# A graph kernel's matrix passes: which operand is TensorE's weights, and how the matrix lies in DRAM

## Chip, core and metric

The kernel runs on one core of a Trainium2 chip. The metric is the time on the device in microseconds (us) of one execution; the median over several executions is given. Profiles are of one execution each.

## The reference

Four graph layers run one after the other on 6250 nodes of 64 features, over 206,250 edges sorted by destination (each node has also a self loop). All of them apply the same adjacency between nodes; only the third also uses data of the edges:

```python
h = relu(layernorm(x)); x = x + sgconv(relu(sgconv(h, W3, b3)), W4, b4)   # two applications of the adjacency
h = relu(layernorm(x)); x = x + D^-1/2 A D^-1/2 h                         # one
h = relu(layernorm(x)); x = x + edge_layer(h, edge_attr, src, dst)        # gather, gate, square, sum, root
h = relu(layernorm(x)); x = x + (h + P h + P P h + P P P h) / 4           # three (P = D^-1/2 A D^-1/2)
```

sgconv sums norm[src] * norm[dst] * x[src] into dst and multiplies by W. edge_layer turns each edge's 64 attributes by two small layers into a scale and a shift, applies them to a projected row Vp[src], and takes for each node the root of the mean of squares.

## The kernel before, in words

The kernel builds the matrix A of edge counts (6272 x 6272 bf16, nodes padded to NB = 49 blocks of 128) once, writes it to DRAM, and then applies it by TensorE. There are CS = 14 strips of CW = 448 destination columns, or NC = 7 chunks of W = 896 columns (CB = 7 blocks). A is symmetric, which the kernel checks during the edge stage. Features are split into three bf16 terms, U3 (or V3) of [128, 49, 3, 64], so that sums keep float32 precision.

The stages are these.

1. The beginning reads the edges, finds where each column begins, and builds the strips: one-hot comparisons on DVE (L935), counts by TensorE (L944), evictions to bf16 by ACT (L948), one DMA a strip (`A<-strip`, L956). The first application of A, `convolve`, runs on each strip while it is in SBUF.
2. Pass 1 and pass 2, both by `gather`, read the matrix back.
3. The edge stage takes 202 groups of 1024 edges. POOL issues eight indirect reads of `v` for each (L1238); PE, ACT and DVE compute the edge layers. In the gaps it compares blocks of A with their transposes (`piece` L1133, `crossed` L1137: PE transposes at L1150, DVE comparisons at L1156 against the tile `there`) and sums the first of the last three applications as far as node rows are done (`partial`, L1162, into Y).
4. The end finishes that first application with the last seventh of each strip (loop at L1412), and then calls `gather` twice (passes 3 and 4), the last of which writes the output.

`gather` (L972) works by strip: seven pieces of seven blocks are read by SP's queue (L980), and for each block `spread` (L736) multiplies three times: the weights are U3[:, b, k, :] (128 x 64), and A's block row (128 x 448) streams through. The three products alternate between the two halves of the PSUM partitions, so p_sum holds two partial sums of the transposed result, features by nodes. ACT evicts it to y (L983); `to_nodes` (L729) multiplies by `twice`, two identities above each other, which adds the halves and turns the chunk back to nodes by features (L733, in float32). p_sum has two buffers. Then a function for each pass goes on with the chunk: `convolved` (L995), `turned` (L1017, with PE work at L725, L1027, L1032), `propagated` (L1388). `split` (L705 to L709) makes the next U3.

The tile framework's scheduler sets the order on every engine, and tracks which buffer waits for which reader; only in the edge stage is the order on PE, ACT and DVE written out by hand (`slot`). [...] The pools for the pieces have 16 buffers of 784 KB in passes 1 and 2 and 12 in the end; a pass's pool is closed before the next one is opened.

Of the kernel before, what the change touches and what calls it, by code (L numbers as in the profile page):

```python
# [8 lines left out]
F32 = mybir.dt.float32  # L9
BF16 = mybir.dt.bfloat16  # L10
# [6 lines left out]
P = 128  # L17
# [598 lines left out]
def fast(ctx, tc, bad, x, src, dst, edge_attr, W3, b3, W4, b4, w1, b1, w2, b2, Bw, Bb, Cw, Cb,  # L616
# [7 lines left out]

    A = [dram.tile([P, NB, CW], BF16, name=f"A{c}") for c in range(CS)]
    pairs = dram.tile([EP + 512, 2], F32, name="pairs")
# [26 lines left out]
    def diagonal(m, name):  # L653
# [4 lines left out]
        return t  # L658

    node = ctx.enter_context(tc.tile_pool(name="node", bufs=1))  # L660
    stat = ctx.enter_context(tc.tile_pool(name="stat", bufs=2))
# [87 lines left out]
    with ExitStack() as ph:  # L749
# [70 lines left out]
        with ExitStack() as ps:  # L820
# [107 lines left out]
            for s in range(CS):  # L928
# [24 lines left out]
                for steps in beside:  # L953
                    for _ in steps:
                        pass
                nc.sync.dma_start(A[s], strip)  # L956
                beside = [convolve(s, strip)]
# [11 lines left out]

    PB = 7  # L970

    def gather(apool, wpool, psum, U3, then):  # L972

        for s in range(CS):
            if s % 2 == 0:
                y = wpool.tile([P, W], F32, name="y")
            p = psum.tile([P, 512], F32, name="p_sum", bufs=2)
            for k in range(NB // PB):
                t = apool.tile([P, PB, CW], BF16, name="piece")
                nc.sync.dma_start(t, A[s][:, k * PB:(k + 1) * PB, :])  # L980
                for b in range(PB):
                    spread(p, U3, k * PB + b, t[:, b, :], CW)
            nc.scalar.activation(y[:, s % 2 * CW:(s % 2 + 1) * CW], p[:, :CW], AF.Copy)  # L983
            if s % 2:
                then(s // 2, to_nodes(psum, y, CB))

    with ExitStack() as ph:
        wpool = ph.enter_context(tc.tile_pool(name="wpool", bufs=2))  # L990
        U3 = of_nodes(node)
        with tc.tile_pool(name="apool", bufs=16) as apool, \
                tc.tile_pool(name="ps1", bufs=1, space=PSUM) as psum:

            def convolved(c, y):  # L995
                z = wpool.tile([P, CB, D], F32, name="z")
                nc.scalar.activation(z, y, AF.Copy)
                add_whole(z, V3, c)
                nc.vector.tensor_mul(z, z, over_features(norm0[:, blocks(c)]))
                nc.vector.tensor_add(z, z, over_blocks(b4_r, CB))  # L1000
                nc.vector.tensor_add(X[:, blocks(c), :], X[:, blocks(c), :], z)
                h = wpool.tile([P, CB, D], F32, name="h")
                normed_and_split(h, U3, c, norm3)

            gather(apool, wpool, psum, V3, convolved)

# [6 lines left out]

        with tc.tile_pool(name="apool", bufs=16) as apool, \
                tc.tile_pool(name="ps2", bufs=1, space=PSUM) as psum:

            def turned(c, y):  # L1017
                z = wpool.tile([P, CB, D], F32, name="z")
                nc.vector.tensor_mul(z, y, over_features(norm3[:, blocks(c)]))
                nc.vector.tensor_add(X[:, blocks(c), :], X[:, blocks(c), :], z)  # L1020
# [8 lines left out]
                nc.vector.scalar_tensor_tensor(aT, aT, 0.2, aT, op0=OP.mult, op1=OP.max)  # L1029
                p_v = psum.tile([P, CB, D], F32, name="p_v", bufs=2)  # L1030
                for k in range(CB):
# [6 lines left out]

            gather(apool, wpool, psum, U3, turned)

# [8 lines left out]
    with ExitStack() as ph:  # L1049
# [83 lines left out]
        def piece(i, s):  # L1133
            held[s % 2] = piece_pool.tile([P, CB, CW], BF16, name="piece")
            nc.sync.dma_start(held[s % 2], A[s][:, blocks(i), :])

        def crossed(n, i, k, b):  # L1137
            if b % ROWS == 0:
                held["there"] = mpool.tile([P, ROWS, 2, CW], BF16, name="there", bufs=2)
                m = min(ROWS, CB - b)  # L1140
                for h in range(2):
                    nc.sync.dma_start(held["there"][:, :m, h, :],
                                      A[2 * i + h][:, k * CB + b:k * CB + b + m, :])

            p = ps_a.tile([P, 512], F32, name="p_sum", bufs=2).bitcast(BF16).rearrange(
                "p (a q) -> p a q", q=P)[:, :CB, :]
            for q in (slice(0, P),) if b != CB // 2 else (slice(0, D), slice(D, P)):
                half, lo = divmod(b * P + q.start, CW)
                for a in range(CB):
                    nc.tensor.transpose(p[q, a, :], held[half][:, a, lo:lo + q.stop - q.start],  # L1150
                                        ident_b)
            there = held["there"][:, b % ROWS].rearrange("p h w -> p (h w)")

# [225 lines left out]
    with ExitStack() as ph:  # L1379
        apool = ph.enter_context(tc.tile_pool(name="apool", bufs=12))  # L1380
        wpool = ph.enter_context(tc.tile_pool(name="wpool", bufs=2))
# [3 lines left out]
        for layer in range(3):  # L1385
# [23 lines left out]
            if layer:  # L1409
                gather(apool, wpool, psum, U3, propagated)  # L1410
            else:
                for s in range(CS):  # L1412
                    t = piece_pool.tile([P, CB, CW], BF16, name="piece")
                    nc.sync.dma_start(t, A[s][:, blocks(NC - 1), :])
                    p = psum.tile([P, 512], F32, name="p_sum", bufs=2)
                    for b in range(CB):
                        spread(p, U3, NB - CB + b, t[:, b, :], CW, NB - CB, CB)
                    nc.vector.tensor_add(Y[:, s, :], Y[:, s, :], p[:, :CW])
                    if s % 2:
                        propagated(s // 2, to_nodes(  # L1420
                            psum, Y[:, s - 1:s + 1, :].rearrange("p s w -> p (s w)"), CB))
# [42 lines left out]
```

## Time and profile before

| | us |
|---|---|
| timed, median of 3 | 4243.05 (4241.24 to 4245.13) |
| the profiled execution | 3727.58 |
| its span | 3725.9 |
| pass 1 (614.14 to 832.44) | 218.30 |
| pass 2 (835.05 to 1082.46) | 247.41 |
| edge stage (1124 to 3226) | 2102.00 |
| first layer of the end | 47.53 |
| passes 3 and 4 | 420.64 |

The profiled execution is 515 us shorter than the timed ones. Its page gives for the whole span PE 3092.7 us busy (83%), DVE 1890.3 (51%), POOL 1666.7 (45%), ACT 1282.9 (34%), and a mean granted TensorE clock of 0.905. Matmul spans overlap in the pipeline: a group's busy time is the time that at least one of them was under way, and its mean is that of one, with its way through the array. DMAs moved 650.35 MB in 278,027 packets; those of the matrix's pieces (`piece<-A`, 498 of 784 KB) took a median of 8.7 us from issue to landing, those of the strips (`A<-strip`, 14 of 5488 KB) 16.5 us.

### The profile page before, as it was taken

What the parts mean: (1) busy time and instruction counts of PE and PEld (TensorE: products, weight loads), DVE (VectorE), ACT (ScalarE), POOL (GpSimd) and SP (SyncE); (2) the same over time, 40 slices, a digit from 0 to 9 for tenths busy, and PEclk for the clock granted to TensorE, in tenths of its full rate; (3) what the DMA queues carried; (4) which work ended last, traced back from release to release, by engine and by line L of the source; (5) the groups of instructions that cost most, each with busy time, mean ns of one, the idle gap of its engine ahead of it and who ended that gap; (6) DMA issues with size and microseconds to landing.
All of it is one profiled execution on the core that took longest, in us unless ns stands there. A gap on an engine that the chain in (4) does not pass through costs nothing.

```text
span 3725.9 us, 57673 instructions
## 1 busy us (share of the span) xinstructions
PE 3092.7 (83%) x23299; PEld 1853.5 (50%) x23299; DVE 1890.3 (51%) x3525; ACT 1282.9 (34%) x2108; POOL 1666.7 (45%) x1870
## 2 busy tenths in 40 slices
PE   0499998999967777888878788787888887799999
PEld 0366665555544444444444444454444444466665
DVE  5999992221214555555655655555555565530100
ACT  0477772001103334433433443443443443210000
POOL 4100000000006777777777777777777777400000
PEclk9999998999987887888888888888888888899999
DMA  3244445968894333344344334334333433499997
GB/s 108 82 183 183 182 184 245 421 270 334 332 188 142 87 88 83 104 110 129 87 119 121 103 104 119 105 102 119 103 108 107 129 104 99 147 350 376 355 357 310
DMA packets 278027, 650.35 MB, mean 175 GB/s; under 512 B 106506, under 2 KB 158788, under 8 KB 275700
## 3 DMA queue, kind: packets, MB, share of 16 engines
q1 hardware_dynamic: 220036, 584.91, 43.4%
q0 software_dynamic: 54112, 58.92, 8.1%
q8 instruction: 185, 3.03, 0.3%
q10 hardware_dynamic: 3600, 2.73, 0.3%
q14 instruction: 94, 0.76, 0.1%
HBM read 562.82 MB, written 83.58 MB: 173 GB/s over the span
## 4 chain that ended last, share of the span: by engine, by line
PE 35%; POOL 32%; issue 14%; DMA 9%; DVE 8%; ACT 2%; POOLq 0%; DVEq 0%; ACTq 0%; SPq 0%
POOL v L1238 32%; PE p_sum L742 26%; DMA v<-Vp_dram,src_g 6%; PE p_a L944 3%; PE p_node L733 2%; DVE hd L935 1%; DVE lo L935 1%; PE p_bc L1264 1%; DMA dst_g<-in_dst 1%; DMA piece<-A 1%; DVE m L1273 0%; DVE m L1274 0%; PE p_node L915 0%; DVE junk L849 0%; PE p_node L725 0%
## 5 line engine op out<-in xcount | busy, mean ns | idle before, releaser
L1238 POOL DMA_INDIRECT v<-Vp_dram,src_g x1616 | 1606.2, 994 | 529.1 <-issue 460.8
L742 PE MATMUL p_sum<-piece,U 128*64 128x448 bf16 x10290 | 1051.7, 360 | 20.0 <-issue 9.9
L742 PEld LDWEIGHTS <-U 128*64 128x64 bf16 x12348 | 694.9, 111 | 527.5 <-issue 95.5
L1264 PE MATMUL p_bc<-BC,h 128*128 128x256 f32 x1616 | 603.6, 509 | 0.0
L1273 DVE TENSOR_TENSOR m<-gate,v 128x512 f32<-128x512 f32 x202 | 140.0, 693 | 798.1 <-DMA v<-Vp_dram,src_g 567.5
L1260 PE MATMUL p_bc<-BC_b,ones 3*128 3x512 bf16 x404 | 182.0, 450 | 359.4 <-DVE m L1274 358.8
L1280 ACT ACTIVATE m<-m 128x512 bf16<-128x512 f32 x202 | 127.3, 630 | 990.7 <-DVE m L1275 990.7
L1090 POOL MEMSET origin<- 128x1 f32 (+1 forms) x194 | 6.5, 96 | 970.8 <-PE p_sum L742 970.8
L1264 PEld LDWEIGHTS p_bc<-BC,h 128*128 128x128 f32 x1616 | 349.7, 240 | 157.6 <-issue 117.1
L1260 PEld LDWEIGHTS <-ones 3*128 3x128 bf16 x404 | 37.5, 93 | 613.6 <-DVE m L1274 486.2
L948 ACT ACTIVATE strip<-p_a 128x784 bf16<-128x784 f32 x392 | 301.7, 820 | 90.0 <-PE p_a L944 88.6
L1250 PE MATMUL p<-h,w_d 128*128 128x512 f32 x404 | 222.6, 633 | 50.7 <-ACT h L1254 50.7
L983 ACT ACTIVATE y<-p_sum 128x448 f32<-128x448 f32 x56 | 30.4, 543 | 678.1 <-PE p_sum L742 678.1
L1254 ACT ACTIVATE h<-p,b_c 128x512 f32<-128x512 f32 x404 | 255.0, 684 | 3.5 <-PE p L1250 3.4
L935 DVE TENSOR_TENSOR lo<-count,key 128x2048 bf16<-128x2048 bf16 x196 | 239.7, 1223 | 0.0
L742 PE MATMUL p_sum<-strip,U 128*64 128x448 bf16 x2058 | 236.2, 358 | 0.4 <-ACT strip L948 0.4
L1156 DVE SCALAR_TENSOR_TENSOR junk<-p_sum,there 128x896 bf16<-128x896 bf16 x196 | 212.3, 1083 | 12.1 <-PE p_e L1246 9.9
L944 PE MATMUL p_a<-hd,lo 128*128 128x98 bf16 x3136 | 189.5, 214 | 33.3 <-DVE lo L935 31.9
L1250 PE MATMUL p<-eT,w_d 128*128 128x512 f32 x404 | 212.3, 608 | 0.0
L944 PEld LDWEIGHTS <-lo 128*128 128x128 bf16 x3136 | 160.0, 101 | 103.4 <-DVE lo L935 81.5
L1391 DVE TENSOR_TENSOR z<-p_node,norm 128x448 f32<-128x448 f32 x21 | 13.1, 625 | 390.3 <-PE p_node L733 390.3
L1292 PE MATMUL p_s<-m,to 128*128 128x192 bf16 x1616 | 202.7, 278 | 1.1 <-DVE r_s L1300 0.4
(177 smaller groups left out, 3191.8 us busy)
## 6 DMA issues: line engine op xcount, KB each, us to landing
piece<-A SPq DMA_DIRECT2D x498, 784.0 KB, 8.7
A<-strip SPq DMA_DIRECT2D x14, 5488.0 KB, 16.5
e<-in_edge_attr SPq DMA_DIRECT2D x202, 256.0 KB, 2.8
v<-Vp_dram,src_g POOLq DMA_INDIRECT x1616
there<-A SPq DMA_DIRECT2D x56, 448.0 KB, 3.9
there<-A SPq DMA_DIRECT2D x56, 336.0 KB, 5.2
pairs<-pair SPq DMA_DIRECT2D x1, 1616.0 KB
Vp_dram<-v SPq DMA_DIRECT2D x7, 224.0 KB, 2.3
```

Of the source, the lines that this page charges most:

```text
L742: nc.tensor.matmul(p[half * D:(half + 1) * D, :w], U3[:, b, k, :], at_block, start=(i < 2), stop=(i >= 3 * n - 2))
L935: nc.vector.tensor_tensor(t, of.unsqueeze(1).to_broadcast(t.shape), key[:, k, at:at + GB].rearrange("p (h j) -> p h j", j=GQ) .unsqueeze(2 ...
L944: nc.tensor.matmul(p[:, j, :2 * NB], lo[:, g // GQ, :, g % GQ], hd[:, g // GQ, :, g % GQ], start=True, stop=True)
L948: nc.scalar.activation(strip[:, :, col:col + 2 * SG].rearrange("p b (j l) -> p b j l", l=2), p[:, :, :2 * NB].rearrange("p j (b l) -> p b ...
L1156: nc.vector.scalar_tensor_tensor(junk, p.rearrange("p a q -> p (a q)"), 0.0, there, op0=OP.add, op1=OP.not_equal, accum_out=unlike[:, n:n ...
L1238: nc.gpsimd.indirect_dma_start(out=v[:, j, :], out_offset=None, in_=Vp_dram[:, :], in_offset=bass.IndirectOffsetOnAxis(ap=src_g[:, g, j:j ...
L1250: nc.tensor.matmul(of[g][p], w, of[g].pop(x), start=True, stop=True)
L1254: nc.scalar.activation(of[g][t], of[g].pop(p), **how)
L1260: nc.tensor.matmul(p_bc[:, 4 * b:4 * b + 4].rearrange("p j o f -> p (j o f)"), ones, BC_b, start=True, stop=False)
L1264: nc.tensor.matmul(p_bc[:, 2 * q:2 * q + 2].rearrange("p j o f -> p (j o f)"), h2[:, q * P:(q + 1) * P], BC, start=False, stop=(k == 1))
L1273: nc.vector.tensor_mul(m, of[g].pop("gate"), of[g].pop("v"))
L1292: nc.tensor.matmul(p, to[:, :, j], m3[:, j].rearrange("p t f -> p (t f)"), start=(j == 0), stop=(j == J - 1))
```

## The change

The matrix lies in DRAM by chunks of 896 columns, not by strips of 448; a strip is written into half of a chunk's rows, and the edge stage's readers take it from there. `gather` works by chunk, with the roles of the operands exchanged: a block of A (128 x 128) is TensorE's weights, and the three terms of a block of U3, side by side (128 x 192), stream through. Since A is symmetric, the product is that of the chunk's own nodes, nodes by features, with the three terms in three columns of 64. Seven destination blocks accumulate in four PSUM banks, two to a bank (the last bank has one), over all 49 source blocks. Each bank is opened by a matmul of zeros that sets both halves, and all products then add to it. Four reduces on DVE add the three terms into z. p_acc has one buffer (the pool's default)[...]; p_v goes from two buffers to one. The eviction y and `to_nodes` leave `gather`, but stay in the loop of the first layer of the end, which now reads whole chunks from the deeper pool. Pieces are twice as large and half as many are held.

```diff
-    A = [dram.tile([P, NB, CW], BF16, name=f"A{c}") for c in range(CS)]
+    A = [dram.tile([P, NB, W], BF16, name=f"A{c}") for c in range(NC)]
+
+    def strip_of(s, bs):
+
+        return A[s // 2][:, bs, s % 2 * CW:(s % 2 + 1) * CW]
...
+    zeros = const.tile([P, 6 * D], BF16, name="zeros")
+    nc.vector.memset(zeros, 0.0)
...
-                nc.sync.dma_start(A[s], strip)
+                nc.sync.dma_start(strip_of(s, slice(0, NB)), strip)
...
-    def gather(apool, wpool, psum, U3, then):
-
-        for s in range(CS):
-            if s % 2 == 0:
-                y = wpool.tile([P, W], F32, name="y")
-            p = psum.tile([P, 512], F32, name="p_sum", bufs=2)
-            for k in range(NB // PB):
-                t = apool.tile([P, PB, CW], BF16, name="piece")
-                nc.sync.dma_start(t, A[s][:, k * PB:(k + 1) * PB, :])
-                for b in range(PB):
-                    spread(p, U3, k * PB + b, t[:, b, :], CW)
-            nc.scalar.activation(y[:, s % 2 * CW:(s % 2 + 1) * CW], p[:, :CW], AF.Copy)
-            if s % 2:
-                then(s // 2, to_nodes(psum, y, CB))
+    def gather(apool, psum, U3, then):
+
+
+        for c in range(NC):
+            p = psum.tile([P, 4, 512], F32, name="p_acc")
+            for k in range(NC):
+                t = apool.tile([P, CB, W], BF16, name="piece")
+                nc.sync.dma_start(t, A[c][:, blocks(k), :])
+                for d in range(CB):
+                    if k == 0 and d % 2 == 0:
+                        nc.tensor.matmul(p[:, d // 2, :6 * D], ident_b, zeros,
+                                         start=True, stop=False)
+                    for b in range(CB):
+                        nc.tensor.matmul(
+                            p[:, d // 2, d % 2 * 3 * D:(d % 2 + 1) * 3 * D],
+                            t[:, b, d * P:(d + 1) * P],
+                            U3[:, k * CB + b, :, :].rearrange("p t f -> p (t f)"),
+                            start=False, stop=(k == NC - 1 and b == CB - 1 and d in (1, 3, 5, 6)))
+            z = stat.tile([P, CB, D], F32, name="z")
+            for q in range(4):
+                n = min(2, CB - 2 * q)
+                nc.vector.tensor_reduce(
+                    z[:, 2 * q:2 * q + n, :],
+                    p[:, q, :n * 3 * D].rearrange("p (d t f) -> p d f t", t=3, f=D),
+                    axis=AX.X, op=OP.add)
+            then(c, z)
...
-        with tc.tile_pool(name="apool", bufs=16) as apool, \
+        with tc.tile_pool(name="apool", bufs=8) as apool, \
...
-                p_v = psum.tile([P, CB, D], F32, name="p_v", bufs=2)
+                p_v = psum.tile([P, CB, D], F32, name="p_v")
...
-            nc.sync.dma_start(held[s % 2], A[s][:, blocks(i), :])
+            nc.sync.dma_start(held[s % 2], strip_of(s, blocks(i)))
...
-                held["there"] = mpool.tile([P, ROWS, 2, CW], BF16, name="there", bufs=2)
+                held["there"] = mpool.tile([P, ROWS, W], BF16, name="there", bufs=2)
                 m = min(ROWS, CB - b)
-                for h in range(2):
-                    nc.sync.dma_start(held["there"][:, :m, h, :],
-                                      A[2 * i + h][:, k * CB + b:k * CB + b + m, :])
+                nc.sync.dma_start(held["there"][:, :m, :],
+                                  A[i][:, k * CB + b:k * CB + b + m, :])
...
-        apool = ph.enter_context(tc.tile_pool(name="apool", bufs=12))
+        apool = ph.enter_context(tc.tile_pool(name="apool", bufs=6))
...
                 for s in range(CS):
-                    t = piece_pool.tile([P, CB, CW], BF16, name="piece")
-                    nc.sync.dma_start(t, A[s][:, blocks(NC - 1), :])
+                    if s % 2 == 0:
+                        whole = apool.tile([P, CB, W], BF16, name="piece")
+                        nc.sync.dma_start(whole, A[s // 2][:, blocks(NC - 1), :])
+                    t = whole[:, :, s % 2 * CW:(s % 2 + 1) * CW]
```

## The prediction

> **What bounds the kernel now.** I read the page's slices first, for the stages, then the stretches of each stage, then the timeline of one chunk in the last passes, since a stage is decided by its own last wait.
>
> ```profile
> PE   0499998999967777888878788787888887799999
> PEclk9999998999987887888888888888888888899999
> DMA  3244445968894333344344334334333433499997
> GB/s 108 82 183 183 182 184 245 421 270 334 332 188 142 87 88 83 104 110 129 87 119 121 103 104 119 105 102 119 103 108 107 129 104 99 147 350 376 355 357 310
> ```
>
> One slice is 93 us. The four passes over the matrix are the slices with both PE and DMA near full: two near 614 to 1082 us, two at the end. The stretches say it exactly (length, then busy time of PE, PEld, DVE, ACT, POOL, clock, DMA share, GB/s):
>
> ```profile
> 614.14:832.44 218.30, 217.31 (x2156) 131.54 (x2156) 53.62 (x96) 19.58 (x38) 0.00 (x0) 0.99 0.87 357
> 835.05:1082.46 247.41, 242.14 (x2293) 142.93 (x2293) 44.65 (x77) 23.83 (x46) 0.00 (x0) 0.99 0.80 320
> 1124.00:3226.00 2102.00, 1681.14 (x8476) 977.49 (x8476) 1175.12 (x2312) 848.33 (x1447) 1605.83 (x1616) 0.85 0.39 107
> 3249.88:3297.41 47.53, 46.61 (x397) 30.02 (x397) 26.34 (x44) 6.92 (x12) 0.00 (x0) 0.95 0.91 330
> 3297.41:3718.05 420.64, 420.60 (x4309) 256.21 (x4308) 35.54 (x58) 24.43 (x44) 0.00 (x0) 1.00 0.92 357
> ```
>
> The last two passes have PE busy 420.60 of 420.64 us at full clock: **PE bounds them**, not the matrix reads, which were seen at 421 GB/s (slice 7) and run at 357 here. The timeline gives the period of a chunk (two strips), from 3297.41 to 3327.49 = 30.08 us:
>
> ```profile
> 3297.41 27.80 PE L742 MATMUL p_sum<-piece,U 128*64 128x448 bf16 x290
> 3325.14 0.88 PE L733 MATMUL p_node<-twice,y 128*128 128x64 f32 x6
> 3325.96 0.57 PE L742 MATMUL p_sum<-piece,U 128*64 128x448 bf16 x3
> 3326.45 1.11 PE L733 MATMUL p_node<-twice,y 128*128 128x64 f32 x8
> 3327.49 27.81 PE L742 MATMUL p_sum<-piece,U 128*64 128x448 bf16 x291
> ```
>
> So 294 matmuls of 448 columns take about 28.0 us, 95.3 ns each, and turning the chunk back to nodes (L733) about 2.0 us, with no idle: p_sum has two buffers, so the eviction (y, 0.54 us on ACT) runs under the next strip. The edge stage (2102 us) is paced by POOL: 1616 indirect reads of 994 ns and about 0.30 us of issue between them are 2091 us. It holds no gather.
>
> **The skill.** The Trainium skill, TensorE: Matmul & The Clock Gate, "Back-to-back issue gap", prices an isolated warm matmul at N/2.4 + 2.5 ns, but a stream of weight loads and matmuls at 81 ns for N=128 and 131 ns for N=512. This trace sides with the first: two 448-column matmuls on the two column halves take 190.6 ns, formula 189.2, and the weight-load streams below run at 56 ns for 128 columns. The same page, Part 1, says that the clock halves after about a 3.4 us window of idleness; here an idle PE of 2.25 to 2.75 us ahead of L1260 was followed by a slow matmul in 2 of 23 cases. PSUM — Partial Sum Buffer, "The four PSUM rules", says that a start flag clears the written-bits of the whole bank: two open groups can't each use one. That is why zeros open each bank; nothing in this trace shows it.
>
> **The change, part by part.**
>
> *Matmuls.* A chunk gets 7 pieces x 7 destination blocks x 7 source blocks = 343 matmuls of 192 columns, each with its own 128x128 weight load, for 294 of 448. The trace has this very shape at L1292, and 128-column ones at L1150:
>
> ```profile
> 3010.05 0.83 PE L1292 MATMUL p_s<-m,to 128*128 128x192 bf16 x8
> 3010.72 0.60 PE L1246 MATMUL p_e<-ident,e 128*128 128x128 f32 x4
> 3012.01 0.56 PE L1150 MATMUL p_sum<-ident_b,piece 128*128 128x128 bf16 x7
> 3012.40 1.08 PE L1250 MATMUL p<-h,w_d 128*128 128x512 f32 x2
> ```
>
> Eight of 192 take 0.67 us from start to start of the next group, 84 ns each with the change of group; seven of 128 take 0.39, 56 ns. The load is hidden. I take 82.5 ns (192/2.4 + 2.5): 343 x 0.0825 = 28.3 us. Bounds: 80 ns from below (the columns alone at the page's 2.4 GHz, 27.4 us); 89 ns from above (the page's stream prices interpolated, 30.5 us).
>
> *Zeros.* Four matmuls of 384 columns a chunk at 162 ns by the same formula: +0.65 us. Bounds 0.6 and 0.8.
>
> *Removed.* Both evictions of y and the 7 L733 products: −2.0 us of PE a chunk in all four passes (L733 stays in the first layer of the end).
>
> *The new wait.* p_acc fills four PSUM banks and has one buffer. In the changed program the first of the four reduces waits for the chunk's last matmul, and the next chunk's first zero load waits for the last reduce. So PE stands still meanwhile. The nearest row:
>
> ```profile
> L1300 DVE TENSOR_REDUCE r_s<-p_s 128x64 f32<-128x192 f32 x202 | 70.8, 351 | 0.2 <-PE p_s L1292 0.2
> ```
>
> 192 elements take 351 ns; the step from there to 448 in 617 ns (L694) is 1.04 ns an element, so 384 take about 550. Three of 550, one of 351, 0.04 us between: 2.13 us. The last matmul's drain (0.24 us from its start at L1292), 0.04 to DVE and 0.13 back to PE give 2.5 us less one slot: **2.48 us of idle PE a chunk**. Bounds: 2.2 (if the two-block reduce costs no second startup) and 3.2. Behind the wait on PE's queue stand the next chunk's 347 matmuls, in pass 2 also the transposes L725 and what follows; on SP's queue the next reads, which wait for PE to free pieces. Six or eight buffers of 4.0 us hold those: a piece of 1568 KB needs 3.8 us at 420 GB/s and its 49 matmuls 4.04, so DMA hides, as now. If the reads fell below 357 GB/s, they would pace it instead.
>
> A chunk then takes 28.3 + 0.65 + 2.48 = **31.43 us**.
>
> *By pass.* Last two: 14 x (31.43 − 30.08) = +18.9. First: period 30.94 now (677.71 to 708.65), 7 x 0.49 = +3.4. Second: 35.9 now; its extra 5.8 (transposes, p_a, p_v and a 0.87 us wait for h) stays, since h is still about 5.4 us of DVE chain and PE has about 4.6 us of work ahead of it: 7 x 1.35 = +9.5. The halved p_v buffer costs nothing: its reader ends 0.6 us after it, a chunk ahead.
>
> *Starts.* The first piece is twice as large: +1.9 us (784 KB at 420 GB/s) at the heads of passes 1 and 2. In the first layer of the end, seven double pieces come from the deeper pool; 0.9 us of piece waits go, PE stays otherwise: −0.5, bounds −1 and +4. The end's tail: 2.13 of reduces for 1.84: +0.3.
>
> *Clock.* 2 of 23 such gaps cooled PE; 26 boundaries x 0.09 x 2 us = +4. Bounds 0 and 65 (all of them, at the 2.5 us that the first strip at 614 lost, 30.63 for 28.1).
>
> *Strips by halves of a chunk.* A strip's write falls from 128 runs of 43.9 KB to 6272 of 896 bytes. The reads into there have 896-byte packets and land 448 KB in 3.9 us; with about 2 of that fixed (Vp_dram's 224 KB lands in 2.3), 5488 KB need about 25 us for 16.5. Strips come 33 us apart with two buffers, and the last is written at 578.3 while its reader starts at 609.8: hidden; above 31 us the excess shows. The edge stage's 92 piece reads get 896-byte packets also, and there goes from two DMAs to one: SP issues 112 there reads before and 56 after, its e reads wait behind less. POOL paces the stage, so I take 0. From both sides: POOL's floor is 1616 x (0.944 + 0.30) = 2010, so at most −90; crowding adds perhaps 1.5 us x 92 of DMA time at a share of 0.39, at most +30.
>
> *Sum.* 18.9 + 3.4 + 9.5 + 3.8 − 0.5 + 0.3 + 4 = **+39 us**: 3727.6 becomes 3767. The three timed runs have a median of 4243.05, 515 us above this profiled execution, and the trace does not say where. I carry the sum over one to one: **4282**. If the 515 were spread over the 46,600 PE instructions (11 ns each), the 2200 added ones would make it 24 more; if over all time, 5 more.
>
> **Rivals.**
> 1. *Small packets speed the edge stage* (faster). Indirect rows now queue behind packets of 6272 bytes; DVE waits 567.5 us for v at L1273, POOL rows stretch from 944 to 994 ns. Interleaved with 896 bytes, they could come earlier. It wins once the stage loses over 47 us of its 2102. At −65: 4217. Against: POOL, not the landing, sets the slot. 0.14.
> 2. *PE stream or boundary dearer*: 89 ns (+62), or the clock falls at most boundaries (+60): about 4344. For it, the page's stream price and the half-clock matmuls in the edge stage; against, L1292 and L1150. 0.17.
> 3. *Weight loads not hidden*: 101 ns at L944, half exposed, gives 343 x 28 x 0.05 = +480: 4760. L1150 speaks against. 0.03.
> 4. *Reads pace the passes in timed runs*: the wait hides under them and nothing moves, 4243. Nothing in the trace for it but the unexplained 515. 0.06.
>
> **How the numbers follow.** The forecast (4260 to 4320) has 0.60. Slower than by 0.2%, which is about what a measurement here can tell from no change (8.5 us): 0.60 + 0.17 + 0.03 = 0.80; within it 0.06; faster 0.14. The range 4236 to 4350 leaves out most of rival 1 and rival 3.
>
> **What would show it.** Right: chunk periods near 31.4 us in the last passes, four reduces near 550, 550, 550 and 351 ns back to back with PE idle about 2.5 us beside them and at clock 1.0 after, 82 to 84 ns a matmul, edge stage within 10 us of 2102. Wrong: a period under 30.1, reduces that start before the chunk's last matmul, or an edge stage that moves by more than the passes do.

## The result and the profile after

| | timed, median (range) | ratio to the kernel before |
|---|---|---|
| before | 4242.32 (4229.53 to 4258.43), 20 runs | |
| changed | 4245.65 (4233.15 to 4264.97), 20 runs | 1.0011, 95% interval 0.9997 to 1.0025 |

The forecast was +39 us; measured are +4.7 us by the ratio (−1.3 to +10.6 by its interval), which can't be told from no change. The edge stage of the whole kernels took about 2.10 ms in some sessions and about 2.55 ms in others, for every kernel alike, so times are compared within one session.

The slices of the changed kernel's page, one slice being 106 us, show the same stages as before. The edge stage is longer and its clock lower, which by the first experiment has nothing to do with the change.

```profile
PE   0599999999566667776777777777777776789998
PEclk9999999999776777877778778778777877899999
DMA  3264579688622223332323333233323323279996
GB/s 103 78 202 161 186 257 416 271 353 342 85 73 71 77 72 87 89 101 77 91 80 98 88 89 93 77 87 88 99 72 89 108 78 87 73 269 366 361 374 275
```

Stretches of the changed kernel (length, then busy time of PE, PEld, DVE, ACT, POOL, clock, DMA share, GB/s) for a stretch inside pass 1, the edge stage, and passes 3 and 4:

```profile
615.00:825.00 210.00, 198.93 (x2363) 195.68 (x2362) 65.65 (x123) 9.21 (x19) 0.00 (x0) 1.00 0.87 357
1132.00:3706.00 2574.00, 1850.06 (x8377) 997.80 (x8378) 1182.31 (x2280) 857.43 (x1432) 1611.47 (x1616) 0.77 0.32 86
3799.10:4235.00 435.90, 403.44 (x4813) 396.92 (x4810) 59.06 (x113) 8.07 (x14) 0.00 (x0) 1.00 0.87 344
```

PE was busy for all of passes 3 and 4 before; now it stands for 32.5 us of 435.9, the boundaries and the last chunk's tail together. The timeline at a chunk's boundary shows where:

```profile
4009.79 1.75 DVE L998 TENSOR_REDUCE z<-p_acc 128x128 f32<-128x384 f32 x4 [25.36 <-PE p_acc L990]
...
4011.59 0.10 PEld L987 LDWEIGHTS <-ident_b 128*128 128x128 bf16 x1 [2.07 <-DVE z L998]
4011.60 0.34 PE L987 MATMUL p_acc<-zeros,ident_b 128*128 128x384 bf16 x1 [1.84 <-DVE z L998]
```

The four reduces stand behind the last product and the next zeros behind the fourth reduce, as forecast, but all four take 1.75 us from first start to last end, and PE is idle for 1.84. The chain of waits (the work that ended last, in order of time) gives the period:

```profile
3984.92 24.85 PE p_acc L990 x301
...
4009.79 1.76 DVE z L998 x4
...
4015.89 24.85 PE p_acc L990 x301
```

It is 30.97 us, against 30.08 before and 31.43 in the forecast. 301 products in 24.85 us are 82.6 ns each (forecast 82.5), and after the idle time the clock is 1.00. The group row of the reduces, for comparison with L1300 in the prediction:

```profile
L998 DVE TENSOR_REDUCE z<-p_acc 128x128 f32<-128x384 f32 x112 | 49.0, 500 | 662.1 <-PE p_acc L990 662.1
```

112 reduces of 500 ns on average would be 56 us one behind the other, but they keep DVE busy for 49.0: they overlap.

### The profile page after: what moved, and what is told of

Read it like the earlier page. It is cut to its first block, busy times and chain, and to the rows that moved or that the text cites. A ratio compares the mean times of both kernels' runs of the same rounds, so it can differ in the third digit from the quotient of the medians.

```text
span 4236.1 us, 59414 instructions
## 1 busy us (share of the span) xinstructions
PE 3243.7 (77%) x24391; PEld 2170.9 (51%) x24391; DVE 1963.8 (46%) x3638; ACT 1267.0 (30%) x2045; POOL 1672.1 (39%) x1870
## 4 chain that ended last, share of the span: by engine, by line
PE 53%; DVE 13%; issue 12%; another core or an unknown queue 10%; ACT 5%; POOL 3%; DMA 3%; DVEq 0%; ACTq 0%; POOLq 0%; SPq 0%
PE p_acc L990 18%; PE p_sum L749 8%; PE p_bc L1277 7%; PE p L1263 6%; POOL v L1251 3%; PE p_a L951 3%; PE p_s L1305 3%; PE p_bc L1273 2%; PE p_e L1259 2%; PE p_sum L1163 2%; DVE m L1286 2%; ACT h L1267 1%; DMA v<-Vp_dram,src_g 1%; DVE m L1287 1%
## 5 line engine op out<-in xcount | busy, mean ns | idle before, releaser
L990 PE MATMUL p_acc<-U,piece 128*128 128x192 bf16 x9604 | 817.4, 247 | 4.3 <-DMA piece<-A 4.0
L990 PEld LDWEIGHTS <-piece 128*128 128x128 bf16 x9604 | 798.1, 98 | 17.8 <-issue 5.6
L1277 PE MATMUL p_bc<-BC,h 128*128 128x256 f32 x1616 | 555.2, 464 | 64.9 <-issue 62.2
L749 PEld LDWEIGHTS <-U 128*64 128x64 bf16 x4116 | 236.3, 113 | 402.2 <-issue 282.3
L749 PE MATMUL p_sum<-piece,U 128*64 128x448 bf16 x2058 | 309.4, 389 | 158.0 <-issue 155.4
L998 DVE TENSOR_REDUCE z<-p_acc 128x128 f32<-128x384 f32 x112 | 49.0, 500 | 662.1 <-PE p_acc L990 662.1
L1263 PE MATMUL p<-h,w_d 128*128 128x512 f32 x404 | 265.8, 739 | 96.8 <-ACT h L1267 76.4
L1305 PEld LDWEIGHTS <-to 128*128 128x128 bf16 x1616 | 179.5, 150 | 219.5 <-issue 213.6
L1263 PE MATMUL p<-eT,w_d 128*128 128x512 f32 x404 | 263.5, 734 | 33.0 <-issue 21.7
L1293 ACT ACTIVATE m<-m 128x512 bf16<-128x512 f32 x202 | 127.3, 630 | 429.4 <-DVE m L1288 292.3
L1350 ACT ACTIVATE m<-m 128x512 bf16<-128x512 f32 x202 | 127.2, 630 | 429.3 <-DVE m L1349 307.0
```

The source lines that it names most:

```text
L749: nc.tensor.matmul(p[half * D:(half + 1) * D, :w], U3[:, b, k, :], at_block, start=(i < 2), stop=(i >= 3 * n - 2))
L990: nc.tensor.matmul(p[:, d // 2, d % 2 * 3 * D:(d % 2 + 1) * 3 * D], t[:, b, d * P:(d + 1) * P], U3[:, k * CB + b, :, :].rearrange("p t f - ...
L1263: nc.tensor.matmul(of[g][p], w, of[g].pop(x), start=True, stop=True)
L1277: nc.tensor.matmul(p_bc[:, 2 * q:2 * q + 2].rearrange("p j o f -> p (j o f)"), h2[:, q * P:(q + 1) * P], BC, start=False, stop=(k == 1))
L1305: nc.tensor.matmul(p, to[:, :, j], m3[:, j].rearrange("p t f -> p (t f)"), start=(j == 0), stop=(j == J - 1))
```

## Experiments

### Where the 515 us are, and which part of the change does what

`e_before` is the kernel before once more. `e_layout` has the matrix by chunks with the gather of before. `e_gather` has the new gather with the matrix by strips, two DMAs to a piece. `e_banks` is the changed kernel with four tiles of one bank for p_acc, so that each bank is released by its own reduce.

```diff
 e_layout, against before:
-                nc.sync.dma_start(t, A[s][:, k * PB:(k + 1) * PB, :])
+                nc.sync.dma_start(t, strip_of(s, slice(k * PB, (k + 1) * PB)))
 (and A, its strips and the edge stage's readers as in the change)
 e_gather, against changed:
-                nc.sync.dma_start(t, A[c][:, blocks(k), :])
+                for h in range(2):
+                    nc.sync.dma_start(t[:, :, h * CW:(h + 1) * CW], A[2 * c + h][:, blocks(k), :])
 (and A and its other readers as before)
 e_banks, against changed:
-            p = psum.tile([P, 4, 512], F32, name="p_acc")
+            p = [psum.tile([P, 512], F32, name=f"p_acc{q}") for q in range(4)]
```

e_before: 

> The kernel before once more, profiled among the timed runs, to find where its 515 us lie. Theory A (the four passes cost as in its first profile, the 515 us lie in the edge stage, whose length in the profile after is 2602 us for 2102): chunk periods 30.1 us in the last two passes and 30.9 and 35.9 in the first two, edge stage near 2600 us, whole 4240. Theory B (the passes are slower than in the first profile, which is why the change cost nothing): chunk periods near 31 us in the last passes, edge stage less by as much.

e_layout: 

> The layout by chunks alone: strips are written into half a chunk's rows, gather is that of before and reads its pieces of 784 KB in runs of 896 bytes. Theory A (the layout costs nothing, the edge stage isn't bound by transfers): ratio to before 0.998 to 1.002. Theory C (896-byte packets and the single read of there shorten the edge stage, which gives back what the passes lose): ratio 0.994 to 0.998, edge stage 10 to 25 us shorter. Theory D (896-byte packets slow the reads of the passes): chunk periods over 30.1 us in the last two passes, DMA share near 1, ratio over 1.003.

e_gather: 

> The exchanged operands alone: the matrix lies by strips as before, gather is that of the change and reads each piece by two DMAs of 784 KB. Theory A: chunk periods as in the profile after (30.97 us for 30.08 in the last passes, 36.43 for 35.9 in the second), so with the later starts +16 to +22 us, ratio 1.004 to 1.005. Theory C: the same +16 to +22, since the gain is the layout's. Theory B: within 5 us of before, ratio 0.999 to 1.001.

e_banks: 

> The change with four PSUM tiles of one bank in place of one of four, so that each bank is reduced as soon as its own last product is in, and PE opens the next chunk while others are reduced. Theory A (PE bounds the passes and the 2.07 us of idle PE a chunk are the wait for the reduces): periods of 28.9 us in the last passes, 28 x 2.07 = 58 us less than the change, ratio to before 0.987 to 0.990. Rival (the reads then pace the passes, at the 344 to 366 GB/s of the profile after): periods over 30.5 us, ratio over 0.997.

Measured beside 4202.66 us for the kernel before: e_before 4213.95 (one run); e_layout 4202.53, ratio 1.0006 (0.9985 to 1.0027); e_gather 4217.93, 1.0026 (1.0003 to 1.0049); e_banks 4170.61, 0.9925 (0.9901 to 0.9948). e_layout lies where theory A had it; e_gather has A's periods, but 11 us by its ratio, less than A's 16 to 22 and more than B's 5.

The rows of the indirect reads (minimum, median and maximum of one in ns, then start of the first and of the last, called first v and last v below) in the first profile of before, in e_before and in the changed kernel:

```profile
L1238 POOL DMA_INDIRECT v<-Vp_dram,src_g x1616: 940/944/1471, 1128.0 to 3225.4; - x180
```

```profile
L1238 POOL DMA_INDIRECT v<-Vp_dram,src_g x1616: 941/947/1453, 1130.5 to 3697.5; - x180
```

```profile
L1251 POOL DMA_INDIRECT v<-Vp_dram,src_g x1616: 938/945/1460, 1132.2 to 3705.3; - x180
```

The stage takes 2097, 2567 and 2573 us; the first reads start within 4.2 us of each other, and the time behind the last is 500.5, 514.7 and 530.8 us. So most of the 515 us lie in the edge stage, which both kernels share. With the same code for this stage e_layout took 2553.8 us and the changed kernel 2573.1, and a difference of 12 us is hard to see behind that.

The passes don't lengthen with it. Their chains in e_before, e_layout and e_gather, two chunks each in pass 3:

```profile
3813.93 27.74 PE p_sum L742 x291
3844.01 27.74 PE p_sum L742 x291
```

```profile
3803.59 27.74 PE p_sum L747 x291
3833.67 27.74 PE p_sum L747 x291
```

```profile
3779.07 24.85 PE p_acc L986 x301
3810.04 24.85 PE p_acc L986 x301
```

The period is 30.08 us in e_before, as in the first profile, and with the new layout alone, and 30.97 with the exchanged operands alone, as in the changed kernel. The exchange of operands is what lengthens the chunks; the layout moves nothing that the times can tell.

In e_banks the timeline has the first two reduces under the chunk's last products and the others beside the next chunk's zeros, and no wait at the boundary:

```profile
729.10 0.56 DVE L998 TENSOR_REDUCE z<-p_acc 128x128 f32<-128x384 f32 x1 [15.35 <-PE p_acc L990]
730.25 0.56 DVE L998 TENSOR_REDUCE z<-p_acc 128x128 f32<-128x384 f32 x1 [0.60 <-PE p_acc L990]
731.41 0.94 DVE L998 TENSOR_REDUCE z<-p_acc 128x128 f32<-128x384 f32 x2 [0.60 <-PE p_acc L990]
...
731.78 0.49 PE L987 MATMUL p_acc<-zeros,ident_b 128*128 128x384 bf16 x2
```

Chunks of 28.95 us follow, 2.02 less: 343 x 82.5 ns and four zeros, nothing else. That is the wait's price, and without it the kernel is faster than both others, though by less than the expected ratio of 0.987 to 0.990: in the last layer the chunks are longer again (last experiment).

### The passes with a short edge stage

To see 12 us, the edge stage was cut in before, changed and e_banks: of its 202 groups only the last of each block of nodes, and no comparison. `nocross` is the kernel before with all groups but no comparison.

```diff
+        few = sorted(set(every.values()))
+        GF = len(few)
-            for i in range(G + ADD_AT):
+            for i in range(GF + ADD_AT):
...
-                            todo.append((crossed, len(crossings), i, k, b))
```

s_before: 

> The kernel before with the edge stage cut short: of its 202 groups only the last group of each block of nodes is computed (about 49), and the comparison of the matrix with its transpose is left out; the four passes over the matrix are whole. It is the yardstick of the three short kernels: the difference of two of them is the difference of their passes, in timed runs. Both theories: the edge stage falls from some 2560 us to between 500 and 900 us, so 2200 to 2600 us in all; the passes keep their periods (30.94, 35.9 and 30.08 us a chunk).

s_after: 

> The changed kernel with the same cut of the edge stage (one group for each block of nodes, no comparison). Theory A (the passes cost in timed runs what their traces show: the two passes of the end 14 x 0.89 = 12.5 us more, the two ahead of the edge stage 2 to 4 us more, and the edge stage swallowed the rest): 15 us over s_before, 11 to 20. Rival B (the timed 4.7 us of the whole kernel is what the passes cost, the trace overstates it): 0 to 8 us over s_before. The forecast's own sum without its clock term was 35 us; it would take 30 or more to save it.

s_banks: 

> The changed kernel with the sums in four tiles of one bank each, and the same cut of the edge stage. Theory A: each of 28 chunks is 2.02 to 2.07 us shorter than in s_after, so 57 us under s_after and some 42 us under s_before. Rival B (only a part of it reaches the time, as the whole kernel's 32 us under the kernel before suggest): 30 to 42 us under s_after.

nocross: 

> The kernel before without the comparison of the matrix with its transpose (196 rounds of seven transposes on TensorE and one comparison on VectorE, and their reads), with all 202 groups. The question is what takes the 470 us by which the edge stage of every timed run exceeds that of the first profile (2567 against 2097 us). Theory A (the pauses of TensorE belong to the groups' own chain): the stage stays between 2400 and 2570 us, and the kernel is at most 170 us faster. Rival B (they belong to the comparison's transposes and their reads): the stage falls to about 2100 us, slots of 10.0 us as POOL's eight gathers set them, and the kernel is 450 us or more faster.

| us | s_before | s_after | s_banks |
|---|---|---|---|
| timed, median of 5 | 2152.87 (2151.97 to 2153.41) | 2164.78 (2163.80 to 2165.08) | 2126.05 (2122.63 to 2127.46) |

The changed passes cost **+11.9 us**, and the ranges don't touch. That lies at the low end of theory A's 11 to 20, and outside rival B's 0 to 8; 35, the forecast without its clock, does not hold. One bank a tile gives 38.7 us under s_after where 28 x 2.02 are 57: rival B's range. The first v comes 25.0 us earlier than in s_after (1101.7 for 1126.7), nearly the whole of 14 waits (28), but behind the last v only 14.1 us are gained. The last group of runs follows that.

nocross: 3721.48 us beside 3724.39 for the kernel before, 0.9993 (0.9987 to 1.0000). Beside these runs the kernel before took 3724 us too, so the long edge stage was not there to be explained; the run shows only that the comparison costs next to nothing in the short one. What makes the stage long in other sessions stays open.

### The whole kernels again, and a first try at the start of pass 1

`r_after` and `r_banks` repeat the changed kernel and e_banks. `s_gather` is e_gather with the cut. `s_start` is s_before with y and z of pass 1 in a pool that is opened behind the pieces' pool.

s_start: 

> The short kernel before (one group for each block of nodes, no comparison), with y and z of the first pass in a pool that is opened behind the pieces' pool, so that the pieces lie where the changed kernel has them. In the trace of the short kernels the first read of pass 1 is issued at 609.1 us in the kernel before, where it waits for VectorE (r, L707), and at 598.4 us in the changed one, where it waits for the last strip's write alone; the first product starts at 613.3 and 608.7. Theory A (the place of the pool decides which tile the first piece overwrites): the first read moves ahead of 600 us, the first product to 608.7 us, and the kernel is 4 to 5 us under s_before (2152.87). Rival B (the wait comes from the layout or the operands' exchange, not from the place): nothing moves, within 1 us of s_before.

s_gather: 

> The short kernel with the operands exchanged and the zeros, but the matrix still by strips (two DMAs a piece). It parts what the gather does from what the layout does. Theory A (the gather's period of 30.97 us is the whole difference, the layout is hidden): within 3 us of s_after (2164.8), first read ahead of 600 us. Rival B (the layout costs or saves something itself): more than 3 us from it, either way.

r_banks: 

> The whole changed kernel with the sums in four tiles of one bank each, again, beside r_after on the same chip. In the short kernel it was 38.7 us under the changed one where 28 waits of 2.07 us would be 58: the trace shows chunks of 28.95 us at first and of 34 to 35 us, with waits for piece reads, in the last two passes. Theory A (reads take over as the bound once the wait is gone): 35 to 42 us under r_after, ratio to the kernel before 0.992 to 0.994. Rival B (the loss came with the cut): 55 to 60 us under r_after.

r_after: 

> The changed kernel again, whole. The kernel before has been timed at 4203 to 4243 us with an edge stage of about 2560 us, and at 3724 us with one of about 2097 us, where runs scatter by a third as much. Theory A (the passes cost 12 us in both kernels' runs, and the first comparison's 4.7 us, -1.3 to 10.6, is this with the edge stage's scatter): 9 to 16 us over the kernel before; if the edge stage is the short one, with an interval that leaves 0 out. Rival B (in the whole kernel the edge stage gives the difference back): within 5 us of the kernel before.

Beside 4202.04 us for before: r_after 4212.78, ratio 1.0019 (1.0001 to 1.0038); r_banks 4159.65, 0.9889 (0.9856 to 0.9922). The interval of r_after holds values of both of its theories. r_banks is 53 us under r_after, between its two expectations, and its interval of some 14 us to either side can't part them; in its trace the first v comes 25.8 us earlier than in r_after and the time behind the last v is 18.1 us shorter, 43.9 in all, and the edge stage between them, which both share, is 10.1 us shorter too. Beside them s_start took 2332.6 us and s_gather 2347.85, which can't be compared with s_before and s_after of the other session, so the times decide none of their theories; only the traces can be read. The first piece of s_gather was read at 598.08 us, that of s_start at 612.55, 31 us behind the issue of the last strip's write as in before. Between the two the passes' difference shows again: 15.3 us by the times, and behind the last v 539.1 us for 527.5, +11.6. s_start moved nothing; it seems that this is because pass 2 kept y and z in the old pool, and so the pool kept its size.

### Start of pass 1 and price of the reduces

`s_start2` moves y and z of both passes. `s_twice` is s_after with each reduce done twice. `s_before_b` and `s_after_b` repeat the two kernels as yardsticks.

```diff
 s_start2, against s_before (pass 1; pass 2 likewise):
+                tc.tile_pool(name="ypool", bufs=2) as ypool, \
-                z = wpool.tile([P, CB, D], F32, name="z")
+                z = ypool.tile([P, CB, D], F32, name="z")
-            gather(apool, wpool, psum, V3, convolved)
+            gather(apool, ypool, psum, V3, convolved)
 s_twice, against s_after:
+                for _ in range(2):
                     nc.vector.tensor_reduce(
```

s_before_b: 

> The short kernel before (one group for each block of nodes, no comparison) again, as the yardstick of the three others of this call. Both theories: 2153 us if the edge stage is the quick one, 2320 to 2345 if it is the slow one; passes as before.

s_after_b: 

> The short changed kernel again beside s_before_b. Theory A (the passes cost the same 12 us whatever the edge stage does): 9 to 15 us over s_before_b. Rival B (the 12 us belong to the quick edge stage, a slow one takes them up): within 6 us of s_before_b.

s_start2: 

> The short kernel before with y and z of both first passes in a pool that is opened behind the pieces' pool, so that the pieces' pool starts where the changed kernel has it (in s_start the second pass kept y and z in the old pool). Theory A (the first piece of pass 1 lay over a tile that VectorE reads to the end of the stage ahead; the place decides): first read issued within 2 us of its strip's write landing, some 10 us earlier than in s_before_b, first product about 4.6 us earlier, time 4 to 5 us under s_before_b. Rival B (the wait doesn't come from the place): first read about 31 us behind the last strip's issue as before, time within 2 us.

s_twice: 

> The short changed kernel with each of the four reduces of a chunk done twice over, one behind the other: eight reduces at each of the 28 boundaries, the same result. Theory A (reduces follow each other at 0.40 us, the time of their 384 elements, and 0.20 for the last, so that the four take 1.75 us from first start to last end): 4 x 0.40 less what the shorter pair saves, 1.4 us more a boundary, 39 us over s_after_b. Rival B (each costs its whole 0.55 us, as the forecast had it, and the 1.75 us come from reduces that start before the chunk's last product): 2.0 to 2.1 us more a boundary, 57 to 60 us over s_after_b.

Measured: s_before_b 2153.86 (2153.04 to 2156.47), s_after_b 2165.15 (2163.34 to 2166.82), **+11.3** this time, s_start2 2146.26 (2145.73 to 2148.66), s_twice 2266.97 (2264.07 to 2267.19). Rival B of s_after_b needs the slow edge stage, which did not come, and was not put to the test.

SP's queue in s_before_b, s_after_b and s_start2, the last strip's write and the first reads of pass 1:

```profile
578.99 0.32 SPq L956 DMA_DIRECT2D A<-strip  x1
610.13 8.43 SPq L980 DMA_DIRECT2D piece<-A  x11
```

```profile
577.82 0.51 SPq L963 DMA_DIRECT2D A<-strip  x1
597.86 22.07 SPq L984 DMA_DIRECT2D piece<-A  x10
```

```profile
578.91 0.32 SPq L956 DMA_DIRECT2D A<-strip  x1
595.64 23.56 SPq L980 DMA_DIRECT2D piece<-A  x19
```

The chains of s_before_b and of s_start2 from there:

```profile
609.43 0.64 DVE r L707
...
610.13 4.34 DMA piece<-A
...
614.61 29.92 PE p_sum L742 x294
```

```profile
608.52 0.63 DVE z L924
...
609.20 30.09 PE p_sum L742 x294
...
641.63 27.74 PE p_sum L742 x291
...
671.71 27.74 PE p_sum L742 x291
```

In the kernel before the first piece's read waits until VectorE is through with r of the stage ahead, and the product for the read's own 4.34 us. With the pool elsewhere it is read 14.5 us earlier, and the first product starts at 609.20 instead of 614.61. The place of the pool decides. The changed kernel, whose y and whose own z in that pool are gone, reads at 597.86 without any such move; s_gather, which has the matrix by strips as before, at 598.08, so it is not the layout. s_start2 gained 7.6 us, more than the 4 to 5 expected: its first products come 5.4 us earlier, and two of its later periods are 30.08 us instead of 30.94. Against s_start2 the changed kernel's passes cost 18.9 us, not 11.3.

The boundary in s_twice:

```profile
1830.29 3.92 DVE L999 TENSOR_REDUCE z<-p_acc 128x128 f32<-128x384 f32 x8 [26.94 <-PE p_acc L990]
...
1834.26 0.50 PE L987 MATMUL p_acc<-zeros,ident_b 128*128 128x384 bf16 x1 [4.02 <-DVE z L999]
...
1834.56 1.81 PE L990 MATMUL p_acc<-U,piece 128*128 128x192 bf16 x10
```

Neither theory gave +101.8 us over s_after_b, 3.6 a boundary. Two things add up. The trace's single records, at another boundary, put the starts of the eight reduces at 0, 0.592, 1.067, 1.649, 2.124, 2.706, 3.181 and 3.562 us: the second of a full-size pair, which overwrites the result of the first, starts 0.58 to 0.59 us behind it, a reduce that doesn't 0.475. By its record the second waits for a semaphore that DVE itself raises, and it starts 0.03 us behind the end of the first (0.56 us); so this is an order that the program sets, and the 0.475 is what two reduces without such a wait show. In s_after_b the four start at 0, 0.474, 0.938 and 1.403, though each of the first three lasts 0.55. So the eight take 3.92 us for 1.75, +2.17; A's 1.4 was wrong because it took pairs for independent, B's 2.1 was near the wait's size but not for B's reason, since no reduce starts ahead of the last product.

The rest is the clock: after 4.02 us of idle PE ten products take 1.81 us, about twice 82.5 ns each, where after 1.84 us of idle time they ran at full speed. Slow products follow at 25 of the 26 boundaries. In passes 3 and 4 the period is 34.98 us on average, 4.0 over s_after_b, of which 2.17 are reduces and some 1.8 clock.

### Where the other half of the wait's gain went

In r_banks the chain of waits of the last pass:

```profile
3944.23 24.27 PE p_acc L990 x294
...
3968.52 0.56 DVE z L998
...
3970.81 0.64 DVE X L1413
3971.47 0.39 SPq L1416
...
3971.95 7.73 DMA piece<-A
...
3979.72 19.82 PE p_acc L990 x238
3999.57 0.56 DVE z L998
...
4030.34 0.56 DVE z L998
```

The reduces at the chunks' ends are 31.05 and 30.77 us apart; all chunks of this pass but the first take 30.4 to 31.0 us, where 28.95 is the period without a wait. The expectations of r_banks and t_out speak of 34 to 35: that is the distance between the places where PE starts again behind a piece, each of which lies 49 products later in its chunk than the one before, and not a chunk's length.

The wait of SP's own queue at the write of out:

```profile
SPq L1416 <- DVE X L1413: 55.3, 3, 19.0
```

SP issues the write of out when X of the chunk is ready, and stands up to 19 us for it with the next pieces' reads behind it; then PE waits for a piece, 4.5 us in the 121 of this stretch. `t_out` lets ACT issue these writes in r_banks, `t_out_before` in the kernel before.

```diff
-                    nc.sync.dma_start(
+                    nc.scalar.dma_start(
                         out[lo:lo + full * P, :].rearrange("(b p) f -> p b f", p=P),
```

t_out: 

> r_banks with the writes of out issued by ACT instead of SP. In the trace of r_banks SP stands up to 19 us at a write of out (it waits for X of its chunk), and the reads of the next pieces behind it; the last layer's chunks then take 34.7 us where the others take 28.95. Theory A (the queue, not the rate of reads, holds them): all 14 chunks of the last two layers at 28.95 us or reads at over 400 GB/s, 20 to 30 us under r_banks, ratio to the kernel before 0.982 to 0.985. Rival B (reads can't go faster than now): chunks stay at a mean of 31 us or more, no gain over r_banks beyond 8 us, ratio 0.989 to 0.993.

t_out_before: 

> The kernel before with the writes of out issued by ACT instead of SP. Theory A (its chunks of 30.08 us are PE's, its reads are ahead by the depth of the pool): no change, ratio 0.998 to 1.002, periods of 30.08 us. Rival B (the wait on SP costs there too): faster by 10 us or more.

Measured beside 4201.23 us for before: t_out 4154.86, 0.9897 (0.9869 to 0.9925); t_out_before 4199.59, 1.0002 (0.9980 to 1.0023). The chain of t_out at the same place:

```profile
3948.92 24.83 PE p_acc L990 x301
...
3977.86 24.83 PE p_acc L990 x301
...
4006.81 24.83 PE p_acc L990 x301
```

Every chunk behind the first of the two passes takes 28.95 us, so by the trace the queue held them, and not the rate of reads. From the last v to the end it is 495.0 us, 21.3 less than in t_out_before beside it, and 11.0 less than in r_banks, whose six longer chunks have 10.5 us over those of t_out. The 20 to 30 that were expected came of the 34 to 35. The times don't show the gain: the ratio is in rival B's range, and that of r_banks in its own session was 0.9889. In the kernel before the queue costs nothing that shows, and its period stays 30.08.

## Why the prediction was wrong

The traces of s_before and s_after, spans 2150.7 and 2163.0, part the difference by stages. Sum 12.3, timed 11.9, and 39 in the forecast, so 27 are missing:

| stage | forecast | measured |
|---|---|---|
| up to the first product of pass 1 | +1.9 | −4.6 (613.3 to 608.7) |
| pass 1, first product to last | +3.4 | −0.6 |
| pass 2, up to its last product | +11.4 | +6.4 |
| first v to last v | 0 | −1.5 |
| last v to the end | +18.7 | +12.6 |
| clock | +4 | 0, apart from the heads |

**Right.** PE bounds the passes, a product takes 82.6 ns with its weight load hidden, four zeros fit 0.65 us, the wait at p_acc is real and shows on PE. The formula on the Trainium skill's page TensorE: Matmul & The Clock Gate, "Back-to-back issue gap", gives 82.5 ns; the page says that a stream of loads and matmuls doesn't follow it, and here it does. The layout by chunks was taken at 0 and e_layout's time shows nothing else; a strip's write took 19.9 us in s_after, where 25 were forecast. The 515 us were carried over one to one, and most of them lie in the edge stage, with the kernel before as with the changed one.

**The step that failed: the wait.** "Three of 550, one of 351, 0.04 us between: 2.13 us" adds durations. The duration was right (0.55 us), but a reduce that depends on nothing still under way starts 0.47 us behind the one ahead, so the four take 1.75. The wait is 2.02 us of the period (30.97 less the 28.95 of e_banks) instead of 2.48, for which the forecast's own terms give 2.46. The period became 30.97 instead of 31.43: 0.46 x 28 = 12.9 us of the missing 27. The page VectorE: DVE Perf Modes, "The DRAIN you can't avoid", says that an operation that is not held starts before the pipe of the one ahead is empty; the runs agree, with a start 0.47 us behind that of a reduce of 0.55. The row at L1300 that the forecast went by gave a duration, and no distance of starts.

**The starts.** +1.9 at pass 1 counted the larger piece, but not when its read could be issued. The trace of before showed the 4.18 us of DMA ahead of 614.14, and r (L707) ahead of that; what was missed is that the read waited there for its buffer, and that this would move with the pools, as s_start2 shows. That is 6.5 us of the difference. At pass 2 the +1.9 came: 6.1 us from the last product to the next instead of 4.1.

**The clock.** 1.84 us of idle time cooled nothing: every period behind the first of passes 1, 3 and 4 is 30.97 us. s_twice shows the other side at 4.02. That agrees with the same TensorE page, Part 1: The HAM clock gate, which asks for an idle window of about 3.4 us. The +4 should have been 0; it came from gaps in the edge stage of before, where the product behind L1260 was slow in 4 of the 23, not in 2, in a stage whose clock was 0.85 in the mean.

**The rest** is small: pass 2's own extra over the bare period, kept at 5.8 us a chunk, fell to 5.5 (36.43 less 30.97); pass 1 came out 0.8 us under the 0.2 that 7 x (30.97 − 30.94) give, for which no run looked; and the edge stage varied.

**The rivals.** Time alone would pick rival 4 ("nothing moves", 0.06), but its mechanism is false: the reads do not hide the wait, and PE stands. The measured 4245.65 us lie within its outer limits of 4236 and 4350, but by luck: no step of its sum leads there. Rival 1 (packets) found no gain in e_layout beyond the 6 us that its interval leaves, rival 3 is out by the 82.6 ns, and rival 2's clock needs a longer idle time than the wait makes.

**What stays open.** 12 us are a ratio of 1.0028: inside the interval of r_after and of e_gather, just outside the first (1.0025). The last layers cost their 12 us beside a long edge stage too (behind the last v 526.6 us in e_gather, 514.7 in e_before), and so do the cut kernels, but whether a long edge stage with all its groups gives some of it back is not shown. Single traces leave it possible: with the new layout that stage took 2553.8 and 2554.9 us (e_layout, e_banks) beside 2567.0 and 2559.3 with the old (e_before, e_gather), and 2553.9 (t_out) beside 2558.6 (t_out_before), but 2560.4 and 2573.1 in other sessions. That is theory C of e_layout, with a few us that the scatter of the times hides.

## What to carry to other kernels

Price a row of short operations by the distance of their starts, not by the sum of their durations, and look in the trace for two neighbours of which one waits for the other and two that don't. The accumulator of four banks with one buffer cost its whole eviction at each boundary; the same banks as separate tiles cost nothing there, and with the wait gone the next one was found on a queue where a write stood in front of reads. Take a period between two equal points of the chunk, not between two ends of a wait. When a pool changes its contents, ask which reader frees the memory under the first buffer of the next one.

## What was not expected of the hardware

The same kernel took 4202 and 3724 us in two sessions, with nearly all of the difference in the edge stage (2567 and 2097 us from the first v to the last), where PE pauses for which the trace names no releaser. Why is open. Idle time of PE of 1.84 us left the products at full speed at each boundary inside a pass; 4.02 us cost some 1.8 us more, with products at half speed.
